# A two-layer graph and feed-forward network on one core: adjacency masks by DMA, fewer small products in the token mixer, six buffers of residual rows

## The chip, the core and the metric

The kernel runs as one program on one NeuronCore of a Trainium2 chip. The metric is the device time of one execution in microseconds (us), and lower is better. Five engines work side by side: TensorE (PE) multiplies matrices, VectorE (DVE) and ScalarE (ACT) do elementwise work and reductions, GpSimd (POOL) does elementwise work and issues DMAs, SyncE (SP) issues DMAs. Each works through its own list of instructions in a fixed order and waits on semaphores where it needs what another engine or a DMA produces.

## The reference, cut to what matters

There are B = 32 graphs of N = 512 nodes with D = 256 features, and an adjacency matrix of 0 and 1 (int32, 32 x 512 x 512). Layer 0 is a message-passing step and a feed-forward step; the change leaves both alone. Layer 1 is a graph attention and a mixer ("hydra"), each behind a layer norm and added to x:

```python
# graph attention, 4 heads of 64; adjacency values are 0 or 1, so one edge type counts
h = einsum('bnd,hde->bhne', ln(x), W)
weight = leaky_relu(e_src[:, :, :, None] + e_dst[:, :, None, :])
attention = softmax(where(adj == 0, NEG, weight), axis=-1)
out = relu(attention @ h + bias) + h;  out = ln_per_head(out);  x = x + out

# mixer: 512 nodes are gathered to 64 slices per head (8 heads), the slices are mixed, and spread back
sw = softmax((x_mid @ W_slice.T + b_slice) / temperature)          # node -> slice weights
st = einsum('bhnc,bhng->bhgc', fx, sw) / (sw.sum(2) + 1e-5)        # 64 tokens of 512
z, xBC, dt = split(st @ in_w.T)          # 512, 512 + 64 + 64, 2 * 8 columns
dt = softplus([dt[:8], flip(dt[8:])] + dt_bias)
x_, Bm, Cm = silu(causal_conv3(xBC))
y = scan forward and backward over the 64 tokens with exp(dt * -exp(A_log)), dt, Bm, Cm, x_
y = (y + x_ * (x_ @ fcD_w.T + D)) * silu(z);  y = y * rsqrt(mean(y*y) + 1e-5) * norm_w
x = x + spread(y @ out_w.T, sw) @ W_out.T + b_out
```

## The kernel before, in words

Layer 0 (`layer0_sorted`) takes the first half of the span. Layer 1 (`layer1_plain`) is built as Python generators whose steps are woven into each other, and the setup of layer 1 is woven into the end of layer 0. The unit of the attention is one graph ("batch", b = 0 to 31); the unit of the mixer is a group g of GB = 2 batches, so there are 16 groups.

For a batch, `prepare(b)` gathers its rows x (L1162, four indirect DMAs on POOL), makes the mask, normalises the rows (`normed`), transposes them on PE (`turned`, L1150 and L1151), and makes the node features `hp` (L1188), from which ACT takes exponentials and a copy `ht` (L1191 to L1194). A row per head, `own`, is written to DRAM and read back on all partitions (L1205 and L1208, SP's queue). `attention(b)` then makes, for each head and each 128 columns, `att = max(own, other) * mask` with one DVE instruction (L1221, in `weigh`) and multiplies it with the features on PE (`avp` L1258, `adp` L1263). `attentions()` weaves `prepare(b + 1)` into `attention(b)` at a ratio of STEPS to TURNS - 4.

`mixer(g)` goes through `slices` for both batches (L1344 to L1364: logits `lgp`, softmax on ACT and DVE, products `yTp`, transposes `swp`), `tokens` (`uTp`, `rnp`), `scan` (below) and `unslice` (`outp` L1576, and the store of the result). The last loop of `layer1_plain` draws the mixer's steps one after the other; each yields a number ("want"), and for each want PACE steps of the attention stream are drawn. This weaving gives the order in which the program is written. Below it the framework's scheduler orders each engine's list once more while building, so the order on an engine can differ somewhat from the written one; it is fixed in the built program.

How the mask is made before: `masks(b)` loads four tiles of 128 x 512 int32 (L1087, SP's queue), and ACT makes a bf16 copy with its row sums (L1101) and the sum of squares (L1102), which together tell whether every value is 0 or 1. PE transposes 16 blocks of 128 x 128 (L1092), and DVE copies four PSUM tiles to a uint8 mask [128, 4, 512] (L1093). At the end of `layer1_plain` the sums become flags (`over`); if any flag is set, a general version of both layers runs instead. It doesn't run here.

`scan(g)` with uT = 128 tokens of two batches (T = 128 columns): `xp` (16 products 128 x 128, L1409); `bcp` (8 products with 64 stationary columns, L1418); `dtp` (16 products with 64 stationary and 8 moving columns, L1437, and 4 with 16 moving columns, L1402); `zp` (4 products with 512 moving columns, L1402); a softplus in small DVE and ACT steps (L1444 to L1454); convolutions of three DVE instructions each (L1426 and L1428), four for xT and two for B and C on 64 partitions; `gp` (L1496), `segp` (L1500), `xtp` (L1505), `qp` (L1510); `yp` (16 products 64 x 64, L1526, the first batch's eight heads first, then the second's); `oTp` (L1544); `msp` (4 products with one moving column, L1552), which carries the mean square of y from a [128, 1] column to a [128, 2] one; `vp` (L1566). PE handles every f32 product as two passes, and the profile counts passes: `xp` stands there with 32 a group.

Residual rows x live in AHEAD_X = 2 * GB + 1 = 5 buffers: `prepare(b)` starts only when batch b - 5 is stored, and where it can't go on it yields True, which sets the credit of the attention stream to 0.

Of the kernel before, what the change touches and what calls it, by code (L numbers as in the profile page):

```python
# [8 lines left out]
F32 = mybir.dt.float32  # L9
F32R = mybir.dt.float32r  # L10
I32 = mybir.dt.int32
# [8 lines left out]
P = 128  # L20
# [844 lines left out]
def layer1_plain(tc, ident, eps, x2s, ranks, adj, w, out, over, ps):  # L865
# [24 lines left out]
    STEPS = 15  # L890
# [4 lines left out]
    AHEAD_X = 2 * GB + 1  # L895
# [5 lines left out]
    with ExitStack() as ctx:  # L901
# [3 lines left out]
        def ctile(name, shape):  # L905
            return cst.tile(shape, F32, tag=name, name=name)

        def const(name, shape, src):
            t = ctile(name, shape)
            nc.sync.dma_start(t, src)  # L910
            return t

        def psum(tag, name):
            return ps.tile([P, N], F32, tag=tag, name=name)
# [3 lines left out]
        identb = cst.tile([P, P], BF16, tag="identb", name="identb")  # L918
        nc.vector.tensor_copy(identb, ident)
# [27 lines left out]
        def add_rows(xt, i):  # L947

            nc.gpsimd.dma_start(xt.rearrange("p t d -> p (t d)"), added[i].partition_broadcast(P), accum_op=ALU.add)

        yield
        edges = ctile("edges", [P, 2, B * NT])
# [7 lines left out]
        bc_w = const("bc_w", [S, 2, KW], w["hy_conv_w"][DI:].rearrange("(c p) k -> p c k", p=S))  # L960
        bc_b = const("bc_b", [S, 2], w["hy_conv_b"][DI:].rearrange("(c p) -> p c", p=S))
        skip = const("skip", [P, H], w["hy_D"].partition_broadcast(P))
        dtb = ctile("dtb", [P, 4, H])
        for i in range(4):
            nc.sync.dma_start(dtb[:, i, :], w["hy_dt_bias"].partition_broadcast(P))
# [31 lines left out]
        with tc.tile_pool(name="raw", bufs=2, side="right") as raw:  # L997
# [4 lines left out]
            for i in range(2):  # L1002
# [7 lines left out]
            pieces = [(dst, w[name], r0)  # L1010
                      for dst, name in ((wfxT, "W_fx"), (inT, "hy_in_w"), (hoT, "hy_out_w"), (owT, "out_w"),
                                        (fcT, "hy_fcD_w"))
                      for r0 in range(0, w[name].shape[0], P)]
# [65 lines left out]
        masked = {}  # L1079

        def masks(b, bank="any"):

            a, raw = [], []

            def load(t):
                raw.append(se.tile([P, N], I32, tag="ai", name=f"ai{b}_{t}", bufs=2))
                nc.sync.dma_start(raw[t], adj[b, t * P : (t + 1) * P, :])  # L1087

            def turn(t):
                pt = ps.tile([P, NT, P], BF16, tag=bank, name=f"maskp{b}_{t}")  # L1090
                for j in range(NT):
                    nc.tensor.transpose(pt[:, j, :], a[t][:, j * P : (j + 1) * P], identb)  # L1092
                nc.vector.tensor_copy(mask[:, :, t * P : (t + 1) * P], pt)  # L1093

            load(0)
            load(1)
            yield
            for t in range(NT):
                n = b * NT + t
                a.append(se.tile([P, N], BF16, tag="a", name=f"a{b}_{t}", bufs=3))  # L1100
                nc.scalar.activation(a[t], raw[t], AF.Identity, accum_out=edges[:, 0, n : n + 1])  # L1101
                nc.scalar.activation(raw[t], raw[t], AF.Square, accum_out=edges[:, 1, n : n + 1])  # L1102
                if t + 2 < NT:
                    load(t + 2)
                if t == 1:
                    mask = se.tile([P, NT, N], mybir.dt.uint8, tag="mask", name=f"mask{b}")
                    yield
                if t > 1:
                    turn(t - 2)
                    yield  # L1110
            for t in range(NT - 2, NT):
                turn(t)
                yield
            masked[b] = mask

        yield from masks(0, "mm")
# [39 lines left out]
        def prepare(b):  # L1156
# [12 lines left out]
            edged = masks(b) if b not in masked else range(3)  # L1169
            for i, _ in enumerate(edged):  # L1170
                if i < 3 or b not in masked:
                    yield
                if i == 2:
                    normed(xt, xn, f"c{b}")
                    add_rows(xt, 0)
                    yield
# [5 lines left out]
            ht = sb.tile([P, NT, AH * HO], F32, tag="ht", name=f"ht{b}")  # L1182
            other = sb.tile([P, NT, AH], F32, tag="other", name=f"other{b}")
# [40 lines left out]
        def attention(b):  # L1224
# [54 lines left out]
            nc.vector.tensor_scalar_max(rs, dt.rearrange("p (t h e) -> p t h e", t=NT, h=AH)[:, :, :, 0], 1e-30)  # L1279
            nc.vector.reciprocal(rs, rs)  # L1280
# [111 lines left out]
        def scan(g, uT):  # L1392
# [7 lines left out]
            def tok_matmul(p, c0, n):  # L1400
                for c in range(KC):
                    nc.tensor.matmul(p, uT[:, c, :], inT[:, c, c0 : c0 + n], start=c == 0, stop=c == KC - 1)  # L1402
# [4 lines left out]
            for k in range(KC):  # L1407
                for c in range(KC):
                    nc.tensor.matmul(px[:, k * T : (k + 1) * T], inT[:, c, DI + k * P : DI + (k + 1) * P],  # L1409
                                     uT[:, c, :], start=c == 0, stop=c == KC - 1)  # L1410
# [3 lines left out]
            pb = psum("any", f"bcp{g}")  # L1414
            for i in range(2):
                c0 = 2 * DI + i * S
                for c in range(KC):
                    nc.tensor.matmul(pb[:S, i * T : (i + 1) * T], inT[:, c, c0 : c0 + S], uT[:, c, :],  # L1418
                                     start=c == 0, stop=c == KC - 1)
            bpad = sb.tile([S, 2, GB, LP], F32, tag="bpad", name=f"bpad{g}", bufs=1)  # L1420
            nc.gpsimd.memset(bpad[:, :, :, : KW - 1], 0.0)
            nc.scalar.copy(bpad[:, :, :, KW - 1 :],
                           pb[:S, : 2 * T].rearrange("p (k j l) -> p k j l", k=2, j=GB))
# [9 lines left out]
            pd = psum("any", f"dtp{g}")  # L1433
            for j in range(GB):
                for i in range(2):
                    for c in range(KC):
                        nc.tensor.matmul(pd[i * G : (i + 1) * G, j * H : (j + 1) * H],  # L1437
                                         uT[:, c, j * G : (j + 1) * G],
                                         inT[:, c, DT0 + i * H : DT0 + (i + 1) * H],
                                         start=c == 0, stop=c == KC - 1)  # L1440
            tok_matmul(pd[:, 2 * H : 4 * H], DT0, 2 * H)
            sp = sb.tile([P, 5, 4 * H], F32, tag="sp", name=f"sp{g}")
            v, e, u, r, dt = (sp[:, i, :] for i in range(5))
            nc.vector.tensor_add(v, pd[:, : 4 * H], dtb.rearrange("p i h -> p (i h)"))  # L1444
# [11 lines left out]
            pz = psum("any", f"zp{g}")  # L1456
            tok_matmul(pz, 0, DI)
            z = sb.tile([P, DI], F32, tag="z", name=f"z{g}", bufs=1)
            nc.scalar.activation(z, pz, AF.Silu)
# [5 lines left out]
            bcT = sb.tile([S, 2, GB, G], F32, tag="bcT", name=f"bcT{g}", bufs=1)  # L1465
            cpad = sb.tile([S, GB, G + 2], F32, tag="cpad", name=f"cpad{g}", bufs=1)
            nc.gpsimd.memset(cpad[:, :, 0 : G + 2 : G + 1], 0.0)
            for i in range(2):
                conv(bpad[:, i], bc_w[:, i, :], bcT[:, i])
                dst = bcT[:, 0] if i == 0 else cpad[:, :, 1 : G + 1]  # L1470
                nc.scalar.activation(dst, bcT[:, i], AF.Silu, bias=bc_b[:, i : i + 1])
# [22 lines left out]
            for j in range(GB):  # L1494
                for i in range(2):
                    nc.tensor.matmul(pg[j * G : (j + 1) * G, i * G : (i + 1) * G], bcT[:, 0, j, :],  # L1496
                                     cpad[:, j, 2 * i : 2 * i + G], start=True, stop=True)
            pl = psum("any", f"segp{g}")
            for j in range(GB):
                nc.tensor.matmul(pl[j * G : (j + 1) * G, :], seg_l, seg[j], start=True, stop=True)  # L1500
# [22 lines left out]
            for j in range(GB):  # L1523
                half = slice(j * G, (j + 1) * G)
                for h in range(H):
                    nc.tensor.matmul(py[half, h * C : (h + 1) * C], heads(mix)[half, h, :],  # L1526
                                     heads(xk)[half, h, :], start=True, stop=True)
# [21 lines left out]
            pm = psum("any", f"msp{g}")  # L1549
            for j in range(GB):  # L1550
                for i in range(P // C):
                    nc.tensor.matmul(pm[i * G : (i + 1) * G, j : j + 1], ident[:, j * G : (j + 1) * G], ms,  # L1552
                                     start=True, stop=True)
            rms = sb.tile([P, GB], F32, tag="rms", name=f"rms{g}")
            nc.vector.tensor_scalar(rms, pm[:, :GB], 1.0 / DI, LN_EPS, ALU.mult, ALU.add)
# [54 lines left out]
        nc.vector.tensor_sub(flags, edges[:, 1, :], edges[:, 0, :])  # L1610
        nc.vector.tensor_scalar(flags, flags, 0.0, None, ALU.not_equal)
        nc.vector.tensor_scalar(edges[:, 0, :], edges[:, 0, :], 0.5, None, ALU.is_lt)
        nc.vector.tensor_add(flags, flags, edges[:, 0, :])
# [635 lines left out]
```

## Time and profile before

| What | Value |
|---|---|
| median of 3 runs | 4320.41 us (4319.69 to 4325.92) |
| the profiled execution's own time | 4319.15 us |
| its span, first to last instruction | 4317.4 us |
| mean granted PE clock | 0.957 |
| busy PE, DVE, ACT, POOL over the span | 3852.3, 3233.1, 2290.3, 1540.2 us |
| last instruction of layer 0 on PE | at 2338 us |
| first start of the mixer's `uTp`, group 0 and group 15 | 2482.4 and 4245.3 us |

One execution is profiled, and all durations below are from it. A group line gives the engine, the line, the operation, output and inputs, the shape, the count, the busy time in us with the mean duration of one instruction in ns, and the idle time of the engine ahead of them with what ended it. A timeline line gives start, length, engine, line, names, and in brackets the idle time ahead. Durations on PE overlap, since products are pipelined: what a run of products costs is read from its start to the start of the next run.

### The profile page before, as it was taken

What the parts mean: (1) busy time and instruction counts of PE and PEld (TensorE: products, weight loads), DVE (VectorE), ACT (ScalarE), POOL (GpSimd) and SP (SyncE); (2) the same over time, 40 slices, a digit from 0 to 9 for tenths busy, and PEclk for the clock granted to TensorE, in tenths of its full rate; (3) what the DMA queues carried; (4) which work ended last, traced back from release to release, by engine and by line L of the source; (5) the groups of instructions that cost most, each with busy time, mean ns of one, the idle gap of its engine ahead of it and who ended that gap; (6) DMA issues with size and microseconds to landing.
All of it is one profiled execution on the core that took longest, in us unless ns stands there. A gap on an engine that the chain in (4) does not pass through costs nothing.

```text
span 4317.4 us, 57903 instructions
## 1 busy us (share of the span) xinstructions
PE 3852.3 (89%) x20311; PEld 2446.7 (57%) x20311; DVE 3233.1 (75%) x7008; ACT 2290.3 (53%) x4756; POOL 1540.2 (36%) x1940
## 2 busy tenths in 40 slices
PE   5567998899999999889998899999999999999997
PEld 4454565566655665555555355565555555565555
DVE  6668877888788977877775777767777777778763
ACT  3344655556655656556664455545554455555432
POOL 2355643664435644354332222222222222222210
PEclk8678999999999999999999999999999999999998
DMA  4557654665546654386542322222222232222210
GB/s 130 161 160 228 191 162 133 192 214 168 149 127 218 197 165 136 109 279 192 153 128 69 78 67 71 79 62 67 74 69 69 76 79 76 75 69 74 62 30 16
DMA packets 260811, 524.16 MB, mean 121 GB/s; under 512 B 39800, under 2 KB 131588, under 8 KB 260509
## 3 DMA queue, kind: packets, MB, share of 16 engines
q0 software_dynamic: 124800, 366.28, 29.5%
q1 hardware_dynamic: 135708, 154.08, 11.4%
q8 instruction: 162, 2.65, 0.3%
q14 instruction: 141, 1.15, 0.1%
HBM read 463.11 MB, written 57.17 MB: 121 GB/s over the span
## 4 chain that ended last, share of the span: by engine, by line
PE 35%; DVE 26%; DMA 10%; issue 9%; POOL 8%; ACT 5%; SPq 0%; POOLq 0%; DVEq 0%; ACTq 0%
PE clsp L623 5%; DVE att L1221 4%; PE gatep L623 4%; PE po L652 3%; PE avp L1258 3%; DVE acc L637 3%; DMA rows<-table,xs 2%; PE yTp L1356 2%; DVE best L599 2%; DMA best<-table,xs 2%; DVE sw L1351 2%; DMA rows<-table,tops 2%; DVE sst L1349 2%; DVE sw L1346 2%; PE oTp L1544 1%
## 5 line engine op out<-in xcount | busy, mean ns | idle before, releaser
L623 PE MATMUL clsp<-xnT,wc 128*128 128x512 f32 x1024 | 522.4, 629 | 47.2 <-ACT cls L625 40.3
L623 PE MATMUL gatep<-xnT,wg 128*128 128x512 f32 x1024 | 496.8, 604 | 9.4 <-ACT gate L625 7.4
L652 PE MATMUL po<-wd,acc 128*128 128x256 f32 x2048 | 451.7, 380 | 5.2 <-DVE acc L641 4.3
L652 PEld LDWEIGHTS po<-wd,acc 128*128 128x128 f32 x2048 | 386.8, 190 | 70.7 <-issue 9.1
L1221 DVE SCALAR_TENSOR_TENSOR att<-own,other,mask 128x512 f32<-128x512 f32 x512 | 365.7, 743 | 78.5 <-DMA own<-ownd 78.5
L599 DVE SCALAR_TENSOR_TENSOR best<-rows,xs,best 128x1024 f32<-128x1024 f32 x212 | 271.0, 1280 | 132.6 <-ACT best L593 74.9
L637 DVE SCALAR_TENSOR_TENSOR acc<-past,fld,acc 128x512 f32<-128x512 f32 x448 | 332.1, 744 | 32.5 <-ACT past L636 24.3
L623 PEld LDWEIGHTS gatep<-xnT,wg 128*128 128x128 f32 x1024 | 196.1, 196 | 249.9 <-issue 198.4
L632 ACT ACTIVATE acc<-tz,fld 128x512 f32<-128x512 f32 x256 | 199.0, 777 | 260.1 <-PE tz L630 235.2
L636 ACT ACTIVATE past<-tz,fld 128x512 f32<-128x512 f32 x448 | 291.3, 693 | 73.3 <-DVE acc L637 72.7
L596 POOL DMA_INDIRECT rows<-table,xs x212 | 252.9, 1193 | 188.6 <-DVE best L599 124.8
L623 PEld LDWEIGHTS clsp<-xnT,wc 128*128 128x128 f32 x1024 | 183.7, 200 | 184.6 <-issue 113.3
L435 PE MATMUL pm<-h,adj 128*128 128x258 f32 (+1 forms) x1024 | 182.3, 325 | 98.5 <-DVE keep L428 35.7
L1258 PE MATMUL avp<-att,hv 128*32 128x512 f32 x2048 | 254.9, 603 | 13.9 <-DVE att L1221 13.8
L625 ACT ACTIVATE gate<-gatep,fld 128x512 f32<-128x512 f32 x256 | 175.5, 685 | 158.3 <-PE gatep L623 129.2
L1344 PE MATMUL lgp<-wsl,x4T 128*128 128x512 f32 x512 | 243.0, 613 | 16.6 <-ACT sw L1345 7.2
L1356 PE MATMUL yTp<-sw,x 128*128 128x512 f32 x512 | 237.8, 602 | 18.9 <-DVE sw L1351 18.2
L554 POOL DMA_INDIRECT xs<-rows_of,order x128 | 155.0, 1211 | 266.8 <-DVE acc L637 104.3
L1162 POOL DMA_INDIRECT x<-x2s,ranks x128 | 136.5, 1066 | 297.7 <-DVE att L1221 133.3
L1309 POOL TENSOR_TENSOR mu<-mu,eps 128x16 f32<-128x16 f32 x32 | 111.2, 3475 | 348.1 <-DVE mu L1308 347.9
L1576 PE MATMUL outp<-v,swT 128*128 128x256 f32 x1024 | 227.6, 381 | 0.0
L435 PEld LDWEIGHTS pm<-h,adj 128*128 128x128 f32 x1024 | 152.5, 214 | 123.9 <-issue 73.0
(590 smaller groups left out, 8643.8 us busy)
## 6 DMA issues: line engine op xcount, KB each, us to landing
adj<-in_adj POOLq DMA_DIRECT2D x128, 256.0 KB, 5.6
ai<-in_adj SPq DMA_DIRECT2D x128, 256.0 KB, 2.8
x<-added POOLq DMA_DIRECT2D x64, 512.0 KB, 5.2
own<-ownd SPq DMA_DIRECT2D x128, 256.0 KB, 3.6
rows_of<-keep SPq DMA_DIRECT2D x32, 550.0 KB, 4.3
x<-in_x SPq DMA_DIRECT2D x32, 512.0 KB, 6.6
xs<-bd POOLq DMA_DIRECT2D x32, 512.0 KB, 5.7
x2s<-xs SPq DMA_DIRECT2D x32, 512.0 KB, 3.0
```

The source lines that it names most:

```text
L435: nc.tensor.matmul(pm[:, : c1 - c0], a[:, i, t * P : (t + 1) * P], h[:, i, c0:c1], start=i + c0 == 0, stop=i + 1 == NT and c0 > 0)
L596: nc.gpsimd.indirect_dma_start(out=row, out_offset=None, in_=table, in_offset=bass.IndirectOffsetOnAxis(ap=idxs[:, k : k + 1].bitcast(U32) ...
L599: nc.vector.scalar_tensor_tensor(m, row, vals[:, k : k + 1], m, ALU.add, ALU.max)
L623: nc.tensor.matmul(pf, wf[:, c, f * P : (f + 1) * P], xnT[:, c, :], start=c == 0, stop=c == DC - 1)
L636: nc.scalar.activation(r, z, AF.Relu, bias=fld[:, f, AT + b : AT + b + 1])
L637: nc.vector.scalar_tensor_tensor(y, r, fld[:, f, CH + b : CH + b + 1], y, ALU.mult, ALU.add)
L652: nc.tensor.matmul(po[:, i, :], acc[f][:, t * P : (t + 1) * P], wd[:, f, :], start=f == 0, stop=f == FC - 1)
L1221: nc.vector.scalar_tensor_tensor(e, own[h], other[:, j, h : h + 1], mask[:, j, :], ALU.max, ALU.mult)
L1258: nc.tensor.matmul(pv[p][k * HW : (k + 1) * HW, :], hv[:, j, h, e : e + HW], weighed[b, h, j], **ends)
L1344: nc.tensor.matmul(pf, xnT[:, c, t * P : (t + 1) * P], wsl[:, c, :], start=c == 0, stop=c == DC - 1)
L1356: nc.tensor.matmul(py, xn[:, t, c * P : (c + 1) * P], sw[:, t, :], start=t == 0, stop=t == NT - 1)
L1576: nc.tensor.matmul(po[:, :D], swT[:, k, t * P : (t + 1) * P], v[:, k, :], start=k == 0, stop=k == KC - 1)
```

## The change

- Masks. POOL issues one DMA a batch from the int32 adjacency in DRAM to a bf16 copy in DRAM (`shorten`, casting on the way), two batches ahead. SP issues one transposing DMA a batch from that copy to the mask in SBUF, now bf16 (`turn`), at the start of `prepare(b)`; batch 0's is issued in the setup. The four loads, eight ACT instructions, 16 PE transposes and four DVE copies of `masks(b)` are gone. The check of the values becomes one ACT instruction over the whole mask (the sum of (mask - 0.5)^2, written over `ht` as scratch) and one small DVE instruction that looks for rows without an edge.
- `prepare(b)` has fewer steps, and STEPS goes from 15 to 12, PACE with it.
- `scan`. The columns of in_w are kept in the order dt, z, x, B and C. B and C come from one product with 128 stationary columns; dt and half of z come from one of 272 moving columns, the other half of z from one of 256. The 16 small `dtp` products go: DVE adds move the dt parts to the other partitions. The convolution of B and C runs once on 128 partitions, ahead of those of xT. The products `yp` and `gp` alternate between the two batches, `segp` takes the batches in reverse order. `msp` goes: four DVE instructions move the mean squares.
- AHEAD_X = 2 * GB + 2 = 6 buffers of residual rows.

```diff
-    STEPS = 15
+    STEPS = 12
-    AHEAD_X = 2 * GB + 1
+    AHEAD_X = 2 * GB + 2
...
-        def masks(b, bank="any"):
...
+        def shorten(b):
+            if b < B:
+                short[b] = dr.tile([N, N], BF16, tag="short", name=f"short{b}", bufs=3)
+                tc.keep_in_program_order(nc.gpsimd.dma_start(short[b], adj[b], max_dma_last_dim=8192))
+
+        def turn(b):
+            if b < B:
+                masked[b] = se.tile([P, NT, N], BF16, tag="mask", name=f"mask{b}")
+                nc.sync.dma_start_transpose(masked[b], short.pop(b))
+
+        for b in range(2):
+            shorten(b)
+            yield
+        turn(0)
...
+            if b:
+                turn(b)
+            shorten(b + 2)
...
+            nc.scalar.activation(ht.rearrange("p t e -> p (t e)").bitcast(BF16), mask.rearrange("p t n -> p (t n)"),
+                                 AF.Square, bias=centre, accum_out=edges[:, b : b + 1])
...
+            nc.vector.tensor_scalar(edges[:, B + b * NT : B + (b + 1) * NT],
+                                    dt.rearrange("p (t e) -> p t e", t=NT)[:, :, 0], 0.0, None, ALU.is_le)
...
-            pb = psum("any", f"bcp{g}")
-            for i in range(2):
-                c0 = 2 * DI + i * S
-                for c in range(KC):
-                    nc.tensor.matmul(pb[:S, i * T : (i + 1) * T], inT[:, c, c0 : c0 + S], uT[:, c, :],
...
+            pb, pz = psum("any", f"bcp{g}"), psum("any", f"zp{g}")
+            for c in range(KC):
+                nc.tensor.matmul(pb[:, :T], inT[:, c, DIN - P :], uT[:, c, :], start=c == 0, stop=c == KC - 1)
+            first = 2 * H + DI // 2
+            tok_matmul(pb[:, T : T + first], 0, first)
+            tok_matmul(pz[:, : DI // 2], first, DI // 2)
...
-            for j in range(GB):
-                for i in range(2):
-                    for c in range(KC):
-                        nc.tensor.matmul(pd[i * G : (i + 1) * G, j * H : (j + 1) * H],
...
-            nc.vector.tensor_add(v, pd[:, : 4 * H], dtb.rearrange("p i h -> p (i h)"))
+            nc.vector.tensor_add(v[:, 2 * H :], pd, dtb.rearrange("p i h -> p (i h)"))
+            for i in range(2):
+                for j in range(GB):
+                    half = slice(j * G, (j + 1) * G)
+                    nc.vector.tensor_add(v[i * G : (i + 1) * G, j * H : (j + 1) * H],
+                                         pd[half, i * H : (i + 1) * H], dtb[half, 0, :])
...
+            conv(bpad, bc_w, bcT)
+            for half, dst in ((slice(0, S), bcT[:S]), (slice(S, P), cpad[:, :, 1 : G + 1])):
+                nc.scalar.activation(dst, bcT[half], AF.Silu, bias=bc_b[half])
...
-            for j in range(GB):
-                half = slice(j * G, (j + 1) * G)
-                for h in range(H):
+            for h in range(H):
+                for j in range(GB):
+                    half = slice(j * G, (j + 1) * G)
                     nc.tensor.matmul(py[half, h * C : (h + 1) * C], heads(mix)[half, h, :],
                                      heads(xk)[half, h, :], start=True, stop=True)
...
-                    nc.tensor.matmul(pm[i * G : (i + 1) * G, j : j + 1], ident[:, j * G : (j + 1) * G], ms,
-                                     start=True, stop=True)
-            nc.vector.tensor_scalar(rms, pm[:, :GB], 1.0 / DI, LN_EPS, ALU.mult, ALU.add)
+                    nc.vector.tensor_scalar(rms[i * G : (i + 1) * G, j : j + 1], ms[j * G : (j + 1) * G], 1.0 / DI, LN_EPS,
+                                            ALU.mult, ALU.add)
```

## The prediction

> **What bounds the kernel now.** I read the busy strip first, for the stages, then the busy time by windows in layer 1, then PE's timeline through one group, then the waits and the chain that ended last.
>
> ```profile
> PE   5567998899999999889998899999999999999997
> DVE  6668877888788977877775777767777777778763
> ```
> ```profile
> core 0: us, PE busy (x) PEld busy (x) DVE busy (x) ACT busy (x) POOL busy (x), PEclk, DMA share, GB/s
> 3024.00:3456.00 432.00, 411.67 (x2774) 245.53 (x2775) 328.16 (x738) 224.29 (x574) 113.84 (x104) 1.00 0.27 72
> 3148.00:3266.40 118.40, 112.29 (x763) 68.45 (x763) 86.19 (x197) 59.58 (x155) 29.37 (x28) 1.00 0.26 68
> ```
>
> The change touches layer 1, the right half of the strip. There PE is busy 95% (411.67 of 432 us), DVE 76%, ACT 52%, POOL 26%, DMA 27%. The second window is one group: PE idles only 118.40 - 112.29 = 6.1 us. Groups follow each other every (4245.3 - 2482.4) / 15 = 117.5 us (first and last start of `uTp`). So PE's own work sets layer 1, and what is taken off PE comes off the time as long as nothing else rises to the bound. Busy PE is not PE at its peak, so I price runs of products in the timeline, from start to next start:
>
> ```profile
> 3205.23 3.84 PE L1409 MATMUL xp<-uT,inT 128*128 128x128 f32 x32
> 3209.00 1.96 PE L1418 MATMUL bcp<-uT,inT 128*64 128x128 f32 x16
> 3210.79 1.36 PE L1437 MATMUL dtp<-inT,uT 128*64 128x8 f32 x32
> 3212.08 1.07 PE L1402 MATMUL dtp<-inT,uT 128*128 128x16 f32 x8
> 3213.00 3.68 PE L1402 MATMUL zp<-inT,uT 128*128 128x512 f32 x8
> 3216.51 0.61 PE L1092 MATMUL maskp<-identb,a 128*128 128x128 bf16 x8
> 3217.05 1.07 PE L1258 MATMUL avp<-att,hv 128*32 128x512 f32 x8
> ...
> 3230.36 1.90 PE L1526 MATMUL yp<-xk,mix 64*64 64x64 f32 x32 [0.36 <-DVE mix L1519]
> 3232.18 2.94 PE L1188 MATMUL hp<-wa,x3T 128*128 128x264 f32 x12
> ```
>
> The products stand shoulder to shoulder. The chain agrees in part: in the scan it runs on PE without a break, but in the slices it runs on DVE, and DVE is almost full there:
>
> ```profile
> 3162.85 0.68 DVE sw L1351
> 3163.53 1.13 DVE av L1312
> 3164.66 0.66 DVE att L1221
> 3165.33 1.14 DVE x L1313
> ...
> 3205.30 3.77 PE xp L1409 x32
> 3209.07 1.89 PE bcp L1418 x16
> 3210.96 1.20 PE dtp L1437 x32
> ```
>
> **What the skill says.** (1) "TensorEngine Tiling (Array Packing)", Key Properties: tiles of the array work independently and can run in parallel. The trace agrees: `vp` alternates two 64 x 64 tiles and takes 3.67 us for 32 passes of 256 columns, 115 ns each, against 219 ns for `outp` on the full array (7.01 us for 32). (2) "DMA: Bandwidth & Descriptors", Latency and other measured facts: a transposing DMA moves 261 GB/s; no transposing DMA is in this trace. (3) "TensorE: Matmul & The Clock Gate", Architectural detail: ACT and DVE are strict FIFO. The trace agrees: DVE stood 4.96 us ahead of one `att` waiting for `own`, with other work behind it.
>
> **The change part by part**, per group of two batches; 16 groups.
>
> *Masks, PE.* 32 transposes go. Three runs of 3, 8 and 4 take 0.27, 0.54 and 0.31 us to the next start: 75 ns each, so 2.4 us. (Their busy time, 31.5 us in 11 groups, gives 2.9; I take the lower.)
>
> *bcp.* 16 passes in 1.79 us become 8 passes of the shape of `xp`, at 3.77 / 32 = 118 ns: 0.94. Gain 0.85.
>
> *dtp, zp.* The 32 small passes go, 1.29. The 8 of 16 columns and 8 of 512 (0.92 + 3.51 = 4.43) become 8 of 272 and 8 of 256. `hp` has 264 columns and takes 2.78 / 12 = 232 ns, so 272 take about 239; 256 take 219: 1.91 + 1.75 = 3.66. Gain 0.77.
>
> *yp, gp, msp.* `yp` takes 1.82 us, 57 ns a pass. `rnp` has 64-column passes that alternate halves: 30 in 1.09 us, 36 ns. At that rate 32 take 1.16; gain 0.66, and 0.1 for `gp` (8 in 0.39). If alternating brought nothing, these 0.76 are lost. `msp` takes 0.33. The reverse order of `segp` I cost at nothing: the same four passes in a PE run that follows anyway.
>
> Sum on PE: 2.4 + 0.85 + 1.29 + 0.77 + 0.66 + 0.1 + 0.33 = 6.4 us a group, 102 us in all.
>
> *DVE.* 8 mask copies of 674 ns go (5.4 us), and three convolution steps (0.28 + 2 x 0.34 = 0.96). Added: four dt adds at 0.19 (the row of the one add), three rms steps at 0.16, two edge tests at about 0.15: 1.5. Net -4.8 of 86 us. It falls where DVE is full, so DVE shrinks about as PE does. `att` now reads a bf16 mask: with uint8 it takes 738 ns, and the same instruction with f32 throughout (L637) 744, so bf16 between them costs nothing either way.
>
> *ACT.* 16 instructions go with their accumulator reads, 16 x (0.636 + 0.202) = 13.4 us. The check adds two of 2048 columns: 512 columns take 0.64 and 1024 1.05, so about 1.9 plus 0.2, 4.2 a group; z in two halves adds 0.35 (2 x 0.473 - 0.597). Net -8.9 of 60. The 2.1 us block stands ahead of exponentials and copies that free PSUM; in the built order one of the two stands ahead of the `hp` exponentials, behind which PE has the 7 us of `yTp` as cover. Without the cover it costs up to 2.1 us a batch.
>
> *Casting DMA.* One POOL instruction a batch; the casting load of layer 0 holds POOL 0.58 us. Queued behind it on POOL are the next x gathers and the `rs` steps of the norms; POOL is 74% idle. 1 MB lands in between 6.15 us (the price of "DMA: Bandwidth & Descriptors", Bandwidth) and 22 us (four layer 0 loads of 256 KB at 5.6 each); it is needed two batches, 117 us, later. The DMA share of 27% rises by a few points.
>
> *Transposing DMA.* On SP it stands, in the built order, ahead of `ownd` and `own` of the batch before, and waits until DVE has read the old mask for the last time. For one batch that is about 3167.1 (end of the last `att` of batch 14, in the DVE timeline) with `ownd` due at 3183.5 (SP's timeline), for the other about 3220.5 and 3241.0: leads of 16.4 and 20.5 us. It takes 2.0 us by the 261 GB/s (512 KB), and 38 us if it were as slow as the factor 19 that the same page (Rules for kernel authors) puts between it and an element-wise pattern. I take 4 to 8: hidden. The ACT check needs the mask later still.
>
> *Sixth x buffer.* POOL waited 75 us in 22 batches for a release by DVE:
>
> ```profile
> POOL x L1162 <- DVE x L1578: 75.0, 5, 16.1
> DVE att L1221 <- DMA own<-ownd: 62.2, 11, 7.0
> PE maskp L1092 <- ACT sw L1345: 4.8, 4, 1.3
> ```
>
> PE barely sees it (`lgp` behind DVE's x: 6.1 us in 11 groups), so I credit nothing; the bound is 0.6 us a group. After the last attention product the built order holds the same blocks of products as before, so the tail isn't lengthened; its last scan is spared some 3 us of PE, contained in the sum. PE's waits directly ahead of `maskp` (8.1 us in 11 groups) were waits for a PSUM bank that the next product shares; I let them stay. What is late next is the DVE chain of the slices.
>
> Against the profiled execution: span 4317.4 - 102.4 = 4215.0. The median stands 3.0 above the span (4320.4), so 4218.
>
> *Weaving and setup.* STEPS and PACE shrink with the steps that go; in the built order `prepare` still runs three batches ahead of the slices, as before, so I credit nothing either way; if the fill of some stretch got worse, that is case C. Batch 0's mask work leaves the end of layer 0, where PE is also about nine tenths busy; its 16 transposes are in the sum, and two casting DMAs and one transposing DMA lie there beside layer 0's own transfers (DMA share 0.35 to 0.56), a few us at most, which I leave out.
>
> **The rivals.**
> (B) *Waits shrink too.* DVE and ACT are relieved where the slices wait for them, and POOL for x. If PE's idle falls from 6.1 to 3.5 us a group: another 42 us, 4176. For it: the chain on DVE in the slices. Against: a shorter PE means less cover.
> (C) *DVE becomes the bound of the scan.* The transposes also filled gaps, and in the scan DVE had only some 3.7 us of idle in 33 while PE loses about 5. If half of the gain turns into waits for `att`, `sw` and `mix`: 51 us given back, 4269.
> (D) *Slower: the transposing DMA holds SP's queue.* Beyond 16.4 and 20.5 us it delays `own` one for one, DVE stops at `att` in order, and PE behind it. The gain is gone where (T - 16.4) + (T - 20.5) = 6.4, T = 21.7 us. At T = 25, 13.1 - 6.4 = 6.7 us a group are lost: 4427. For it: no row shows this DMA. Against: that is more than ten times the 2.0 us of the page.
> (E) *The change doesn't do what it says,* the products aren't packed and the waits move one for one: 4318.
>
> **How the numbers follow.** Likeliest (A) 4218, own range 4195 to 4240, chance 0.60; B 0.13; C 0.17; D 0.08; E 0.02. The range 4170 to 4275 takes in B and C and leaves out D and E, and the outer ends of B and C. About 0.2%, 8.6 us, can be told from no change: faster A + B + C = 0.90, same 0.02, slower 0.08.
>
> **What would show it.** Right: groups every 111 us, no `maskp`, no small `dtp`, `yp` in about 1.2 us, a transposing DMA that lands in under 16 us, PE idle near 6 us a group, `own` waits no longer than 7 us. Wrong: `yp` still at 1.8; PE idle of 9 us or more with DVE named in the scan (C); `att` waiting for `own` in every batch (D).

## The result, and the profile after

| What | Before | After |
|---|---|---|
| median of 6 runs | 4325.39 us (4319.69 to 4336.23) | 4351.01 us (4349.18 to 4359.09) |
| ratio after to before, 95% interval | | 1.0063 [1.0047, 1.0078] |
| the profiled execution's own time | 4319.15 us | 4359.09 us (the longest of its six) |
| mean granted PE clock | 0.957 | 0.938 |
| busy PE, DVE, ACT over the span | 3852.3, 3233.1, 2290.3 us | 3809.0, 3178.9, 2188.8 us |
| first `uTp` of group 0 and of group 15 | 2482.4, 4243.7 us | 2501.0, 4285.0 us |

The changed kernel is slower by 0.6%. PE, DVE and ACT have less to do, and the time is longer. Of the 40.0 us between the two spans, 18.6 lie ahead of the first `uTp`, 22.8 in the 15 groups that follow (1761.2 before, 1784.0 after), and the tail is 1.3 shorter. (The 4245.3 us in the table of before is the start of the last instruction of group 15's `uTp`; its first starts at 4243.7.)

The busy strip of the changed kernel, and its busy time in the window of before and in one group, from `uTp` to `uTp`:

```profile
PE   5567998899999999888997899999999999999987
DVE  6668877887788977787775766766767766677663
```
```profile
core 0: us, PE busy (x) PEld busy (x) DVE busy (x) ACT busy (x) POOL busy (x), PEclk, DMA share, GB/s
3024.00:3456.00 432.00, 401.00 (x2414) 242.46 (x2412) 302.50 (x695) 191.76 (x460) 120.56 (x112) 0.96 0.32 76
3100.72:3220.94 120.22, 111.75 (x687) 67.91 (x687) 84.77 (x197) 55.24 (x134) 31.41 (x30) 0.94 0.31 71
```

The strip hardly differs. The windows do: PE idles 31 of 432 us instead of 20, and the column PEclk has gone from 1.00 to 0.96, in this group to 0.94. A group takes 120.2 us with 687 passes where one of before took 118.4 with 763. PE's timeline through the scan shows both losses:

```profile
3109.23 3.84 PE L1397 MATMUL xp<-uT,inT 128*128 128x128 f32 x32
3112.91 1.06 PE L1404 MATMUL bcp<-uT,inT 128*128 128x128 f32 x8
3113.80 2.00 PE L1389 MATMUL bcp<-inT,uT 128*128 128x272 f32 x8
3115.64 1.89 PE L1389 MATMUL zp<-inT,uT 128*128 128x256 f32 x8
3117.36 0.60 PE L1132 MATMUL x3T14p<-ident,hv 128*128 128x128 f32 x4
...
3122.21 1.04 PE L1248 MATMUL adp<-att,hv 128*32 128x512 f32 x8
3127.49 0.69 PE L1478 MATMUL gp<-cpad,bcT 64*64 64x64 f32 x8 [4.24 <-ACT cpad L1448]
3128.11 1.97 PE L1482 MATMUL segp<-seg,seg_l 128*64 128x512 f32 x4
...
3133.37 4.90 PE L1173 MATMUL hp<-wa,x3T 128*128 128x264 f32 x12
3138.20 1.15 PE L1508 MATMUL yp<-xk,mix 64*64 64x64 f32 x32
```

The products are as short as forecast: from `xp` to the transposes behind `zp` 8.13 us, before 11.28. Then PE stands for 4.24 us until `cpad` is there. And what follows the gap is slow: 12 passes of `hp` take 4.83 us to the next start, where before they took 2.78; `segp` takes 1.90, before 1.01. This is PE at half of its clock (the record of the clock has 0.50 for `segp` here). Where the 4.24 us come from, ACT's timeline ahead of `gp` shows (a table load has no tile's name):

```profile
3120.94 1.28 ACT L1430 ACT_TABLE_LOAD   x1
3122.24 0.23 ACT L1430 ACTIVATE sp<-sp 128x32 f32<-128x32 f32 x1
3122.48 1.28 ACT L1448 ACT_TABLE_LOAD   x1
3123.78 0.40 ACT L1448 ACTIVATE bcT<-bcT,bc_b 64x128 f32<-64x128 f32 x1
3124.20 1.28 ACT L1436 ACT_TABLE_LOAD   x1
3125.49 0.23 ACT L1436 ACTIVATE sp<-sp 128x32 f32<-128x32 f32 x1
3125.74 1.28 ACT L1448 ACT_TABLE_LOAD   x1
3127.03 0.40 ACT L1448 ACTIVATE cpad<-bcT,bc_b 64x128 f32<-64x128 f32 x1
```

The softplus (exponential L1430, logarithm L1436) and the two Silus of B and C take turns, and each turn loads another table. `cpad`, the end of this chain (products, DVE's adds and convolutions, ACT), is there 18.2 us after the start of `xp`. In the kernel before it was there earlier, and PE came later:

```profile
3213.19 0.19 DVE L1444 TENSOR_TENSOR sp<-dtp,dtb 128x32 f32<-128x32 f32 x1 [0.28 <-PE dtp L1402]
3221.06 0.38 ACT L1471 ACTIVATE cpad<-bcT,bc_b 64x128 f32<-64x128 f32 x1
3223.20 0.46 PE L1496 MATMUL gp<-cpad,bcT 64*64 64x64 f32 x8
```

`xp` started at 3205.23, so `cpad` was ready after 16.2 us, and PE got to `gp` after 18.0. PE was the longer of the two by only 1.8 us. Now PE's work in this stretch takes 14.0 us, and the chain takes 2.0 us more. That gives the gap: 4.0 us less of PE's work, less 1.8 that PE was behind, plus 2.0, is 4.2. (With the medians of all groups: 2.9 - 1.1 + 2.0 = 3.8.) Why the chain is longer, DVE's timeline of the changed kernel shows:

```profile
3115.71 0.48 DVE L1413 TENSOR_SCALAR xT<-xpad,conv_w 128x128 f32<-128x128 f32 x2
3116.11 1.13 DVE L1415 SCALAR_TENSOR_TENSOR xT<-xpad,conv_w,xT 128x128 f32<-128x128 f32 x4
3117.16 0.48 DVE L1413 TENSOR_SCALAR xT<-xpad,conv_w 128x128 f32<-128x128 f32 x2
3117.55 1.13 DVE L1415 SCALAR_TENSOR_TENSOR xT<-xpad,conv_w,xT 128x128 f32<-128x128 f32 x4
3118.60 0.75 DVE L1206 SCALAR_TENSOR_TENSOR att<-own,other,mask 128x512 f32<-128x512 f32 x1
3119.26 0.17 DVE L1423 TENSOR_TENSOR sp<-bcp,dtb 128x16 f32<-128x16 f32 x1
```

The softplus' first add (`sp`) starts 10.0 us after `xp`, before 8.0. DVE's list now has all four convolutions of xT and one `att` ahead of it, where it had two convolutions. From this add to `cpad` it takes 8.2 us in both kernels. The convolution of B and C, too, is written ahead of those of xT but stands behind them in the built order (from 3120.06). The waits of ten groups:

```profile
PE gp L1478 <- ACT cpad L1448: 38.4, 10, 4.2
PE yTp L1343 <- DVE sw L1338: 16.4, 11, 2.3
```

`gp` waits 3.8 us in each group, before never for `cpad`. Over the 15 groups PE is busy for 1676.5 us before and 1635.0 after, and idle for 84.7 and 148.9. A part of the busy time passes at half clock. Counted from the record of the clock (half of each busy microsecond at half clock is lost), PE lost 10.6 us of its busy time that way before and 72.9 after. So the work itself would take some 1666 and 1562 us at full clock, an estimate from these figures. Of the 104 us of work that went, 64 came back as idle time and 62 as slow clock: +22, measured +22.8.

### The profile page after: what moved, and what is told of

Its sections match the earlier page's. It is cut to its first block, busy times and chain, and to the rows that moved or that the text cites. A ratio compares the mean times of both kernels' runs of the same rounds, so it can differ in the third digit from the quotient of the medians.

```text
span 4357.4 us, 54620 instructions
## 1 busy us (share of the span) xinstructions
PE 3809.0 (87%) x19031; PEld 2416.5 (55%) x19031; DVE 3178.9 (73%) x6973; ACT 2188.8 (50%) x4324; POOL 1598.7 (37%) x1973
## 3 DMA queue, kind: packets, MB, share of 16 engines
q1 hardware_dynamic: 183548, 137.29, 10.7%
## 4 chain that ended last, share of the span: by engine, by line
PE 18%; DVE 18%; DMA 6%; ACT 6%; POOL 5%; issue 4%; SPq 0%; DVEq 0%; POOLq 0%; ACTq 0%
DVE att L1206 5%; PE yTp L1343 2%; PE hp L1173 2%; POOL mu L1296 2%; PE clsp L623 2%; PE gatep L623 2%; DMA x<-x2s,ranks 1%; PE lgp L1331 1%; POOL x L1144 1%; PE avp L1243 1%; DVE sst L1336 1%; DVE sw L1333 1%; PE outp L1556 1%; DMA own<-ownd 1%; DMA ownd<-turned 1%
## 5 line engine op out<-in xcount | busy, mean ns | idle before, releaser
L1206 DVE SCALAR_TENSOR_TENSOR att<-own,other,mask 128x512 f32<-128x512 f32 x512 | 364.4, 739 | 68.4 <-DMA own<-ownd 66.5
L1144 POOL DMA_INDIRECT x<-x2s,ranks x128 | 151.9, 1187 | 344.3 <-DVE x L1558 143.5
```

The lines of the kernel that those rows point to most:

```text
L1206: nc.vector.scalar_tensor_tensor(e, own[h], other[:, j, h : h + 1], mask[:, j, :], ALU.max, ALU.mult)
```

## The experiments

Theory W: the scan and the slices are bound by chains over DVE and ACT, which PE's own work covered; what is taken off PE comes back as waits and, where they are long, as half clock behind them. Theory C is the prediction's rival (DVE is the bound). Theory D puts the loss on the masks' DMAs and the sixth buffer, theory S on the order of instructions at the end of layer 0. The expectations count the runs of this study in the order of the table; each ratio is to the kernel before, timed on the same chip.

| Run | Median us | Ratio, 95% interval | 15 groups, us |
|---|---|---|---|
| e1 masks alone | 4348.84 | 1.0054 [1.0032, 1.0075] | 1779.7 |
| e2 scan alone | 4357.03 | 1.0061 [1.0045, 1.0078] | 1782.5 |
| e3 B and C first on ACT | 4325.24 | 0.9992 [0.9981, 1.0004] | 1765.1 |
| e4 dt, B, C ahead of `xp` | 4298.68 | 0.9934 [0.9915, 0.9953] | 1736.0 |
| e5 five buffers | 4387.27 | 1.0144 [1.0119, 1.0170] | 1819.5 |
| e6 useless products ahead of `gp` | 4302.69 | 0.9934 [0.9912, 0.9957] | 1731.6 |
| e7 masks alone, useless transposes | 4331.36 | 1.0009 [1.0000, 1.0019] | 1764.7 |
| e8 scan alone, dt, B, C ahead of `xp` | 4280.19 | 0.9890 [0.9866, 0.9914] | 1708.8 |
| e9 after, four dt bias loads | 4357.18 | 1.0056 [1.0037, 1.0075] | 1790.0 |
| e10 as e8, four dt bias loads | 4273.21 | 0.9863 [0.9845, 0.9882] | 1709.6 |
| e11 as e4, useless transposes | 4289.59 | 0.9899 [0.9883, 0.9916] | 1709.5 |
| e12 as e4, attention steps moved | 4315.41 | 0.9964 [0.9952, 0.9975] | 1746.7 |

**Each half alone.** e1 takes the masks by DMA, STEPS 12 and the new test of the mask's values onto the kernel before; e2 takes `scan`, the order of the columns of in_w and the constants. Both keep five buffers.

> Masks by DMA alone on the kernel before, with STEPS 12, and five buffers of residual rows; the scan is the old one. Theory W (the loss is in the scan: products were taken out of a stretch, xp to gp, whose length a chain on ACT and DVE sets, so gp waits about 4 us a group and PE's clock halves behind it): the old scan keeps its products, 32 transposes a group of 75 ns go, most of them outside that stretch, so this is faster than before, 4280 to 4310 us, and gp waits under 1 us a group. Theory D (the loss is in the mask's DMAs: small packets, casts beside the gathers, SP's queue): 4340 us or more, slower than before. Theory C (DVE is the bound): 5.4 us of casts a group go, 4240 to 4270 us.

> The scan's part alone on the kernel before (input products, order of the convolutions, yp in turns, mean squares by DVE), with the old masks and five buffers. Theory W: the 4 us that the products lose come back as a wait of gp for cpad of 3 to 4 us a group, and the half clock behind it costs 1 to 3 us more; 4320 to 4360 us. Theory D: the scan's saving of 4 us a group is had in full, 4250 to 4270 us.

Each half alone is slower, by about as much as both together. e2's time is as W said, though the wait is shared and smaller than the 3 to 4 us that I expected at `gp`: `gp` waits 1.4 us a group and `segp` 1.1, and the clock falls to 0.97. e1 is a miss for W as I had stated it, and no proof for D, since the profile names other waits. PE's largest wait and one of DVE's in ten groups:

```profile
PE yTp L1341 <- DVE sw L1336: 40.3, 15, 6.5
DVE av L1297 <- POOL mu L1294: 66.5, 20, 8.6
```

Two things can stand behind it, and e1 doesn't tell them apart. The transposes covered the softmax in the slices: in one group of the kernel before, 16 of the 32 stood around the first batch's logits. And DVE is late with the softmax, because it waits for POOL (see the sixth buffer below); before, this wait was 16.4 us.

**The chain shortened.** e3 puts the Silus of B and C ahead of the exponential on ACT, e4 the products ahead of `xp`:

```diff
 # e3
+            conv(bpad, bc_w, bcT)
+            for half, dst in (...):
+                silu = nc.scalar.activation(dst, bcT[half], AF.Silu, bias=bc_b[half])
...
-            nc.scalar.activation(e, e, AF.Exp)
+            with tc.issue_after(silu.ins):
+                nc.scalar.activation(e, e, AF.Exp)
 # e4: bcp and the product of 272 columns, then xp, then the product of 256
```

> The changed kernel with the convolution of B and C and its two Silus written ahead of the softplus, and the softplus' exponential issued on ACT behind the second Silu, so that ACT switches its table twice less ahead of cpad (2 x 1.28 us). Theory W: gp no longer waits for cpad; the next of the chain, segp, which needs the logarithm, waits 1 to 2.5 us instead, short enough to keep PE's clock in most groups; 4270 to 4320 us, faster than the changed kernel by 30 to 80. Theory D or C: within 10 us of the changed kernel.

> The changed kernel with the products of B and C and of dt and half of z ahead of xp instead of behind it, and so the softplus and the convolution of B and C 3.8 us earlier; the same instructions in another order. Theory W: gp and segp find their inputs ready, the wait of 4 us a group and the half clock behind it are gone, 4 to 7 us a group or 64 to 112 us in all; 4240 to 4290 us. Should the xT chain be next, xtp waits up to 2 us a group, and 4290 holds. Theory D or C: within 10 us of the changed kernel, 4340 to 4360.

e3 is 26 us better than the changed kernel, less than I expected. `gp` still waits 1.2 us a group, the larger wait only went one step on, and it stayed long enough for the clock (0.97):

```profile
PE segp L1483 <- DVE seg L1473: 34.7, 10, 4.2
```

e4 has the same instructions in another order and is 52 us faster, now below the kernel before by 0.7%. `gp` follows `xp` after 10.7 us, and of the waits `segp` keeps 1.2 us a group. The median missed the upper end of W's 4240 to 4290 by 9: the slices' wait for `sw` was still there, and the clock at 0.97.

**The wait and the clock told apart.** e6 adds four products that nobody reads ahead of `gp`:

```diff
+            pf = psum("any", f"fill{g}")
+            for i in range(4):
+                tc.keep_in_program_order(nc.tensor.matmul(pf, ident, uT.rearrange("p c n -> p (c n)"),
+                                                          start=True, stop=True))
             pg = psum("any", f"gp{g}")
```

> The changed kernel with four products without use (ident by uT, 128 x 512, no one reads them) on PE ahead of gp in each group: 8 passes of 0.46 us, 3.7 us of added work. It computes the same output. Theory W with the clock: gp's wait of 3.8 us becomes about 0.3 us, the added work takes its place, and the stretch of half clock behind it goes: gp to yp is 1.5 to 2 us shorter, 24 to 40 us in all, 4310 to 4330 in spite of more work. Theory W without the clock (the wait alone costs): within 8 us of the changed kernel. If PE's work is the bound: 3.7 us x 16 = 59 us slower, 4410.

More work, less time: 48 us faster than the changed kernel, more than the 24 to 40 that I expected. PE's timeline of one group:

```profile
3109.43 3.60 PE L1477 MATMUL fill<-uT,ident 128*128 128x512 f32 x8
...
3119.11 0.45 PE L1481 MATMUL gp<-cpad,bcT 64*64 64x64 f32 x8 [1.66 <-ACT cpad L1448]
```

From `xp` to `gp` it takes 18.25 us (median), in the changed kernel 18.22, though PE's work in between is 2.7 us longer: the added products, less eight passes of `adp` that the built order now has behind `gp`. So the chain sets this stretch and PE's work doesn't. What is gained lies behind it: `gp` to `yp` takes 7.10 instead of 8.96 us although the eight passes have come in, `yp` to `oTp` 4.05 instead of 5.20, at full clock. The clock over the 12 us from the start of `gp`, in e6 and in the changed kernel (the two groups shown):

```profile
3119.11:3131.11 12.00, 10.91 (x96) 7.43 (x97) 5.84 (x14) 10.29 (x32) 3.76 (x4) 1.00 0.35 60
```
```profile
3127.49:3139.49 12.00, 12.00 (x73) 8.90 (x74) 3.87 (x9) 7.79 (x23) 1.00 (x2) 0.58 0.15 26
```

The third figure from the right is the clock: 1.00 against 0.58. So the gap of 4.24 us costs some 5 us more by the clock, 0.42 x 12. Over the 15 groups PE's idle time falls from 149 to 97 us, and the mean clock rises from 0.96 to 0.99.

**The same for the slices.** e7 is e1 with the 16 transposes a batch put back, of the identity, at the four steps of `prepare`; e11 is e4 with the same.

```diff
+            def cover(t):
+                pt = psum("any", f"maskp{b}_{t}").bitcast(BF16)
+                for j in range(NT):
+                    tc.keep_in_program_order(nc.tensor.transpose(pt[:, j * P : (j + 1) * P], identb, identb))
+            cover(0)
             yield
```

> The masks by DMA alone (the first run of this study) with the 16 transposes a batch put back on PE without use: the identity is transposed instead of the mask, nobody reads it, and no cast follows. It computes the same output. Theory W with the clock: PE is never idle for long, so the work that is added, 2.4 us a group, costs nothing or even gains: yTp's wait for sw shrinks and the clock holds; 4310 to 4340, not slower than without the transposes (4349). Theory D (the mask's DMAs cost the time): 38 us on top, 4380 to 4390.

> The changed kernel with dt and B and C ahead of xp (the fourth run, 4299 us, 15 groups in 1736 us) and the 16 transposes a batch put back on PE without use. It computes the same output. Theory W with the clock: yTp no longer waits 2.3 us for sw in a group's first batch and the clock holds, which pays for the added 2.4 us a group: 15 groups in 1715 to 1740 us, 4280 to 4305. If PE's work were the bound there: 15 groups in 1772 us, 4335.

Both medians lie where W said. About 36 us of work are added (2.4 in each of 15 groups), and e7 is 17 us faster than e1, e11 9 faster than e4, there with intervals that touch. In e11 15 groups take 26 us less than in e4, and `yTp` waits for `sw` 11.1 us in them instead of 20.3, but the first `uTp` came at 2511. With six buffers in both, e11 against e4 is the cleaner test of the cover in the slices, as far as one profile of each shows it. In e7 DVE's wait for POOL fell as well, to 35.4 us in ten groups, so what e1 lost isn't missing cover alone. e7 also shows what the casts and ACT's sums were worth: with PE's work as before and 5.4 us of casts a group gone from DVE, the groups take 1764.7 us, before 1761.2. e4 and e6 say the same: they leave DVE's work as it is in the changed kernel and are some 50 us faster. So DVE's busy time wasn't the bound, and theory C falls.

**The sixth buffer.**

> The changed kernel with five buffers of residual rows instead of six. Theory D (the sixth buffer crowds the DMA queues at the start of layer 1, whose first group came 10 us later than the last instruction of layer 0 explains): 8 to 18 us less than the changed kernel, 4333 to 4343. Theory W (the loss is waits of PE in the mixer and the half clock behind them): nothing is won, 4345 to 4365; the gather of the rows comes later, and what it holds up costs up to 10 us.

A miss for both: with five buffers the changed kernel is 36 us slower. The waits of DVE, POOL and PE in ten groups:

```profile
DVE av L1299 <- POOL mu L1296: 64.3, 20, 8.1
POOL x L1144 <- DMA out<-x: 117.3, 13, 18.0
PE yTp L1343 <- DVE sw L1338: 35.0, 12, 6.0
```

POOL's queue is in order. The gather of x waits there for the store that frees the buffer, and the `pow` of the norm stands behind it; DVE waits for that with `av`, the softmax stands behind `av`, and PE waits with `yTp`. e1, with five buffers too, has the same waits (66.5 us of DVE for POOL, PE's longest 6.5); the changed kernel with six has 36.1 us of DVE for POOL. I take it that the gather comes sooner since `prepare` has fewer steps; that was not tried by itself. The sixth buffer alone on the kernel before wasn't tried.

**The end of layer 0.** The dt bias takes two loads instead of four in the setup. With four, two of them unused, the scheduler gives PE and ACT nearly the old order there: in the traces e10 has that of the kernel before, e9 that of e1, up to a few blocks.

```diff
-        dtb = ctile("dtb", [P, 2, H])
-        for i in range(2):
+        dtb = ctile("dtb", [P, 4, H])
+        for i in range(4):
             nc.sync.dma_start(dtb[:, i, :], w["hy_dt_bias"].partition_broadcast(P))
```

e8 is e2 with e4's order of products; e10 is e8 with the four loads, e9 the changed kernel with them.

> The scan's part alone with old masks and five buffers, and with the products of B, C, dt and half of z ahead of xp, as in the fourth run of this study. Theory W: with gp's chain started 3.8 us earlier the scan's saving of 4 us a group is had, 4255 to 4290 us, and faster than the changed kernel so ordered (4299), since the masks by DMA give up PE work that covers yTp's wait. Theory D says the same for another reason (no mask DMAs). If the half clock comes from elsewhere: 4300 to 4330.

> The changed kernel with four loads of the dt bias in the setup as before, of which two are not used, instead of two. Nothing else differs; but with four loads the order of instructions that the scheduler gives to the end of layer 0 on PE and ACT is that of the first run of this study, whose first uTp started at 2489 us, and not that of the changed kernel, 2501. Theory S (the later start of layer 1 comes from the order in layer 0's last stages, where the setup is woven in, not from the masks' DMAs): first uTp at 2486 to 2492, the rest as in the changed kernel, 4336 to 4346. Theory D (the DMAs at the start): first uTp stays near 2501, 4345 to 4360.

> The scan's part alone with old masks, products of dt and B and C ahead of xp (the eighth run, 4280 us, first uTp at 2502) and four loads of the dt bias, of which two are not used. The order on PE and ACT up to the first scan is then that of the kernel before (first uTp at 2482). Theory S: first uTp at 2480 to 2485, the rest as in the eighth run, 4258 to 4266 us, the best so far. If the start depends on something else: 4275 to 4285.

e8 is as W said: the scan's 4.1 us x 15 = 61 are there, of which 52 arrive (1761.2 to 1708.8). S forecast the first `uTp` at 2486 to 2492 us in e9 and at 2480 to 2485 in e10; it came at 2495 and 2498, and both medians are above S's ranges too: misses. The absolute times are a poor measure here, since layer 0 itself, which no edit touches, differs by several us between executions. I count from the burst of `po` products in layer 0 that starts near 1791 us before, near 1797 in the changed kernel and 1805 in e10. From there to the first `uTp` it takes 692 us before, 704 after, 698 in e9; 707 in e8, 693 in e10. By that the order costs about 14 us in e8 and 6 in the changed kernel. e2, with the old masks and two loads, takes 705, so the masks' DMAs aren't needed for it. But e5, with two loads and five buffers, takes 699, so the order isn't the only thing that counts. In the median e10 gains 7 on e8 with intervals that overlap, and e9 can't be told from the changed kernel. These are single profiles that speak for S; the times don't settle it. The other 6 us of the changed kernel's start stay open.

e10 is the fastest found, 1.4% below the kernel before: old masks, the new scan, its chain started first. In the window from 3024 to 3456 us its clock is 1.00 and PE idles 22.8 us, about as before.

**Real work as cover.**

> The changed kernel with dt and B and C ahead of xp, four loads of the dt bias as above, and the attention's steps moved: the mixer asks for less of them ahead of the scan's products (4 becomes 2) and for more between the logits and yTp (5 becomes 6 for each batch), so that real work covers yTp's wait. Theory W: 15 groups in 1700 to 1730 us with the first uTp near 2488, 4258 to 4290 us. If the granularity of the attention's steps undoes the move: 15 groups in 1736 as in the fourth run, 4285 to 4295.

A miss. The built order between the logits and `yTp` is nearly the same as before the move (in the group looked at, the same 28 passes of `avp`, `adp` and `hp` stand ahead of the first batch's `yTp`), and `yTp`'s wait for `sw` grew to 41.9 us in 15 groups from 20.3 in e4. The first `uTp` came at 2509 us, not near 2488. That the steps are too coarse is a guess. Moving wants blindly isn't a way to place cover.

## Why the prediction was wrong

The forecast was 4218 us; the result is 4351, on the other side of no change.

- **The step that failed** is "PE's own work sets layer 1, and what is taken off PE comes off the time", with "The products stand shoulder to shoulder" as its evidence. Products without gaps show that PE was never early, not by how much it was late. From `xp` to `gp` PE's work took 18.0 us and the chain over DVE and ACT beside it 16.2. So 1.8 us could be won there, and the change took 4.0 off PE. The rest, and what the chain itself gained in length (next point), became the wait of `gp`, 3.8 us in each group, with half clock behind it. e6 shows that PE's work isn't the bound: the stretch has the same length with 2.7 us more of it. The timeline of ACT and DVE between the two, which I had, would have told it: `cpad` at 3221.06 + 0.38 and `gp` at 3223.20.
- **The chain itself got longer**, by 2.0 us, and the prediction has no term for that. It priced the steps that DVE and ACT lose and gain, not their order: in the built order the softplus' first add stands behind more of DVE's work. That is about half of the wait. e3 and e4, which start parts of the chain sooner, are 26 and 52 us faster than the changed kernel.
- **The sum on PE, 6.4 us a group, was right.** `bcp`, `dtp` and `zp` lost 3.15 us (forecast 2.91), `yp` 0.74 (0.66), and the masks' transposes went. At full clock the work that went is 6.9 us a group by the estimate above. DVE and ACT lost less busy time than forecast, 3.4 and 5.8 us a group instead of 4.8 and 8.9; why wasn't looked into.
- **That the waits stay** failed too. PE's idle time went from 5.6 to 9.9 us a group. `maskp` was cover for `yTp` in the slices (e11 against e4; in e1 and e7 POOL has a part in it). "What is late next is the DVE chain of the slices" was there as a sentence, without a price.
- **The clock** isn't in the prediction at all. I read 1.00 and took it for given. It is 62 of the 126 us that the waits and the clock cost. The Trainium skill, "TensorE: Matmul & The Clock Gate", HAM oscillation, warns of PE gaps over some 3.4 us. The trace agrees: the 14 gaps of about 4 us ahead of `gp` in the changed kernel are all followed by a mean clock under 0.9 in the next 12 us, of the gaps of 0.9 to 1.7 us 5 of 30. But shorter ones aren't safe: of those of 2.2 to 2.8 us 4 of 5 are followed by it, and in e2, where `gp` and close behind it `segp` wait about 1 us each, it is 10 of 13.
- **Rival C** had the right sign of the mechanism, gain turned into waits in the scan, and the wrong limit: it isn't DVE's busy time (e7) but the order of small steps on DVE and ACT, and the wait is for ACT's `cpad`. It gave back half; all of it and more came back. **D** didn't happen: the transposing DMA holds SP for 2.1 us (median), and the longest wait for `own` is 5.5 us, before 7.0. When it lands isn't in the trace, but no wait names it. **E** didn't: what should go went.

```profile
L1093 SPq DMA_TRANSPOSE mask<-short x32: 1707/2140/3625, 1994.4 to 4076.4; - x32
```

- **Small terms.** The bf16 mask costs `att` nothing (739 ns), as forecast. The test of the mask's values takes 2.00 + 0.19 us, as forecast; ACT also waits ahead of it for the norm of an earlier batch, since it writes over `ht` (62.8 us in all), which the prediction didn't see. Whether that costs time wasn't tried. The sixth buffer, "I credit nothing", is worth 36 us in the changed kernel (e5). Setup, "a few us at most": 12 us more from the burst in layer 0 to the first `uTp`, about half of them by the order of instructions, by one profile (e9).

## What to carry to other kernels

A full engine is a bound only where nothing else is due when it is: before you take work off it, find for each stretch the chain over the other engines that ends with it, and price the stretch as the longer of the two. After the change, look where the chain's first steps stand in the built order. Where work on PE can't be replaced by other work, start the chain earlier first (e4, e8 gained 52 and 77 us on the versions without it), and keep PE's gaps short, since half clock can follow a long one. Test a suspected cover by adding useless work: if the time doesn't grow, PE's work isn't the bound of that stretch.

## What the runs showed of the hardware

- Useless products, 3.6 us a group, made the kernel 48 us faster: they filled idle time, and PE's clock stayed up (0.99 over the 15 groups, instead of 0.96).
- A gap of 4.24 us ahead of `gp` was followed by 12 us at a mean clock of 0.58, a gap of 1.66 us at 1.00. The record of the clock has only 1.0 and 0.5. Over the 15 groups of the changed kernel it has 24 stretches of 0.5: 11 of 3.41 us, 6 of 6.83, 6 of 10.24 and one of 20.48.
- A table load takes 1.28 us on ACT, and the next activation starts right behind it. The Trainium skill, "ScalarE: Activation LUTs", What ACT_TABLE_LOAD costs, gives 1283 ns, which agrees, and a drain of about 1380 ns besides, which this trace doesn't show (0.01 us between the exponential's end and the next load).
- 64 x 64 products that alternate two tiles take 34 ns a pass (`yp`, 1.08 us for 32), in one tile after the other 57. `gp`, with 8 passes, gained nothing by it: 0.38 us in e6, 0.39 before.
